# Layer 0 of a four-layer network: middle taps of ten images read from GpSimd-made copies moved by one element; two dummy products fewer after layer 1

## The chip, the core and the metric

The kernel runs on one core of a Trainium2 chip. The core has five engines that work side by side and wait for one another by semaphores: TensorE (PE in the profile, its weight loads PEld) multiplies matrices into PSUM, VectorE (DVE) and ScalarE (ACT) do elementwise work, GpSimd (POOL) does elementwise work in SBUF and issues DMAs, SyncE (SP) issues DMAs. The metric is the time of one execution on the device in microseconds (us); lower is better.

## The reference, cut to what matters

The input is 16 images of 256 channels, 28 x 28 pixels. Four layers follow one another. Layers 0 and 2 are of one kind: the sign of the input is convolved with the sign of the weights (3 x 3 taps, padding 1), and the result is normalized over all images.

```python
# layer 0
out = sign(x)                                   # the value of _binary_activation
y = conv3x3(out, sign(weights)) * mean(abs(weights))
yn = (y - mean(y)) * rsqrt(var(y) + EPS)        # over images and pixels
x = yn * gamma + beta + x
# layer 1: conv3x3 of sign(x), gates, conv1x1, residuals
# layer 2: x = prelu(bn(binconv2(sign(bn(prelu(binconv1(sign(bn(x)))))))) + x)
# layer 3: attention over the 784 pixels of each image, with a residual
```

The mean and the variance need every image, so a layer's normalization, and with it the next layer, can't start before the last image's convolution has ended.

## The kernel before

Each image lies in SBUF as 128 partitions x 2 channel groups x 784 pixels. sign_layer (L380) runs a signed convolution and is used three times: for layer 0 and for the two convolutions of layer 2. The two halves of the output channels are packed into one fp16 weight (a + 4095 b), so one pass of products yields both.

- sign_image (L424) has ScalarE write the signs of an image into fpads, a padded fp16 tile of 2 x 30 x 30 elements per partition, one of two such tiles in turn. Layer 0's sign0 (L520, instruction at L522) makes two instructions per image, one for each channel group, and then the next load of x is issued on SP.
- products (L390, matmuls at L400) runs over 6 chunks (2 channel groups x 3 rows of taps), the pieces of a block (two halves of 14 rows for a whole image) and the taps c = 0, 1, 2 of a row. The tap is where the read begins in a padded row: element c. So an image has 6 x 2 x 3 = 36 matmuls of 392 columns, and the read of the middle tap begins one 2-byte element into a row of 30.
- With the argument shifted, images from number direct on have the taps in another order: taps 0 and 2 of all chunks first, then the middle taps, which read the tile shifted at element 0. shifted is a copy of fpads moved on by one element, made by a DMA on SP in sign_image (L430). Layer 2 does this, with direct 4 in its first convolution and 2 in its second. Layer 0 gives no shifted tile, so all its taps read fpads.
- apart (L407) takes the packed result out of PSUM: ScalarE's L416 makes b, VectorE's L418 makes a. The result tile of layer 0 is n, 16-bit integers, two buffers in turn (room0). PSUM has three result buffers.
- post0 (L678) takes VectorE's statistics (L682) of the image before and stores n to DRAM (n0d) by a DMA on GpSimd (L684).
- steps are pieces of work that prepare the weights of the later layers. Two of them run beside each whole image, on ScalarE (L324, L343, L346, L588) and VectorE (L325, L577, L592 and the tensor operations recorded at L137).

The order of block j, written out by hand for PE, ScalarE, VectorE and SP, is: products of image j, sign_image of image j + 1, post of image j - 1, steps, apart of image j. GpSimd is not in that list; a planner orders its queue.

Layer 0's call is at L688. Its tiles come from the pool ph; the tag vs belongs to a tile of layer 1 (L717), which is first written after layer 0.

Between the layers PE runs keep_busy(n) (L498, matmuls at L502): n products of 512 columns on a tile of zeros that nobody reads. At the end of layer 1, after the last image's 1x1 convolution, the order is: ScalarE scales the convolution's result (L946), VectorE applies the prelu (L870), PE runs keep_busy(14) at L1175, then PE sums the gate's hidden layer (L709), ScalarE applies its bias (L893), PE makes the gate (L901), ScalarE the sigmoid (L902). VectorE makes layer 2's first variance from it (l_v), ScalarE its square root (L280), and with the result ScalarE writes the first signs of layer 2 (L1228).

Of the kernel before, what the change touches and what calls it, by code (L numbers as in the profile page):

```python
# [39 lines left out]
P = 128  # L40
B = 16
S = 28
# [7 lines left out]
PARTS = HALVES[:-1] + [(B - 1, r, HR // 2) for r in (HR, HR + HR // 2)]  # L50
# [36 lines left out]
def forward(ctx: ExitStack, tc: tile.TileContext, d: dict, out: bass.AP, careful: bool):  # L87
# [3 lines left out]
    nc = tc.nc  # L91
# [18 lines left out]
    SIGNS = FR if careful else F16  # L110

    def sign_pads(pool, tag):

        t = pool.tile([P, 2, 2, S + 2, S + 2], SIGNS, name="fpads", **({"tag": tag} if tag else {}))
        for i in (0, S + 1):
            for edge in (t[:, :, :, i:i + 1, :], t[:, :, :, :, i:i + 1]):
                nc.gpsimd.memset(edge.bitcast(F32) if careful else edge, 0.0)
        return t
# [14 lines left out]
    def vtile(name):  # L133
        return const.tile([P, 2], F32, name=name)

    def tt(o, a, b, op):
        V.tensor_tensor(o, a, b, op)  # L137
        return o
# [157 lines left out]
    def packed_weights(pool, **kw):  # L296
        return pool.tile([P, 6, 3, P], SIGNS, name="wpk", **kw)
# [66 lines left out]
    def whole_images(parts):  # L364

        return parts if careful else IMAGES + parts[2 * len(IMAGES):]

    def pieces(block):

        i, r0, rows = block  # L370
        return [(h, h * HR, HR) for h in range(2)] if rows == S else [(0, r0, rows)]

    def by_halves(ap, block):
        return halves(ap) if block[2] == S else ap

    def first_part(block):

        return 2 * block[0] + (block[1] >= HR) + (block[1] > HR)

    def sign_layer(pads, w, temp, room, sign, post, steps, moments, blocks, together=1, shifted=None, direct=2):  # L380

        pss = [None] * len(blocks)
        abs_ = [None] * len(blocks)

        groups = 2 if careful else 1
        size = 6 // groups

        def products(*js):  # L390
            for j in js:
                pss[j] = conv_ps()
            moved = shifted is not None and blocks[js[0]][0] >= direct
            for taps in ((0, 2), (1,)) if moved else ((0, 1, 2),):
                for n, (k, g) in enumerate(CHUNKS):
                    for j, (h, r0, rows) in ((j, p) for j in js for p in pieces(blocks[j])):
                        r = g + r0
                        for c in taps:
                            src, c0 = (shifted, 0) if moved and c == 1 else (pads, c)
                            T.matmul(  # L400
                                pss[j][:, n // size if careful else h, :rows * S].rearrange("p (a b) -> p a b", b=S),
                                lhsT=w[:, n, c, :], rhs=src[:, blocks[j][0] % 2, k, r:r + rows, c0:c0 + S],
                                start=(n % size == 0 and c == 0),
                                stop=(n % size == size - 1 and c == (1 if moved else 2)),
                            )

        def apart(j):  # L407
            for g in range(groups):
                n = blocks[j][2] * S
                t, ab = temp("t1")[:, :n] if careful else None, room(blocks[j], g)  # L410
                ps = pss[j][:, :, :HN] if blocks[j][2] == S else pss[j][:, g, :n]
                if careful:
                    A.activation(by_halves(t, blocks[j]), ps, AF.Identity, bias=rounding, scale=1.0 / PACK)
                    A.activation(ab[:, 1], t, AF.Identity, bias=unrounding)
                else:
                    A.activation(by_halves(ab[:, 1], blocks[j]), ps, AF.Copy, scale=1.0 / PACK)  # L416
                a, b = (by_halves(ab[:, mo], blocks[j]) for mo in range(2))
                V.scalar_tensor_tensor(a, b, -PACK, ps, ALU.mult, ALU.add)  # L418
                if g == 0:
                    abs_[j] = ab  # L420
                else:
                    tt(abs_[j], abs_[j], ab, ALU.add)

        def sign_image(i):  # L424

            for r0, r1 in ((0, HR + 1), (HR + 1, S)) if i == 0 else ((0, S),):
                load = sign(i, slice(r0, r1), lambda k: inner(pads[:, i % 2], k, r0, r1))
                if shifted is not None and i >= direct:
                    to, of = (t[:, i % 2].rearrange("p k a b -> p (k a b)") for t in (shifted, pads))
                    nc.sync.dma_start(out=to[:, 0:-1], in_=of[:, 1:])  # L430
                if load:
                    load()

        late = None
        gathered = False
        with tc.manual_schedule(engines={ET.PE, ET.Activation, ET.DVE, ET.SP}):
            sign_image(0)
            for j, block in enumerate(blocks):
                if j == 0:
                    products(*range(together))  # L440
                elif together <= j:
                    products(j)
                if block[1] == 0 and block[0] + 1 < B:
                    sign_image(block[0] + 1)
                after = post(blocks[j - 1], abs_[j - 1]) if j > 0 else ()
                if first_part(block) > EARLY and not gathered:
                    gathered = True
                    moments.gather()
                for p in range(len(pieces(block))):
                    if late:  # L450
                        late()
                    step = steps.pop(0) if first_part(block) + p >= 2 and steps else None
                    late = step() if step else None
                apart(j)
                for f in after:
                    f()
            post(blocks[-1], abs_[-1])
        assert not steps and not late

    def inner(pad, k, r0=0, r1=S):  # L460
        return pad[:, k, 1 + r0:1 + r1, 1:S + 1]
# [10 lines left out]
    def block_moments(name, blocks, summed=False):  # L472
        return Moments(name, EARLY, len(blocks) - EARLY, EARLY * HN, summed and not careful)

    sf0, sf1, sf2 = vtile("sf0"), vtile("sf1"), vtile("sf2")
    w0 = packed_weights(wpool, tag="wa")
# [13 lines left out]
    with tc.tile_pool(name="ps_conv", bufs=3, space=PSUM) as psc, \  # L490
            tc.tile_pool(name="ps_sm", bufs=2, space=PSUM) as pss:

        def conv_ps():
            return psc.tile([P, 2, 512], F32, tag="cv", name="cv")
# [3 lines left out]
        def keep_busy(n):  # L498

            ps = pss.tile([P, 512], F32, tag="sm", name="unused")  # L500
            for _ in range(n):
                tc.keep_in_program_order(T.matmul(ps, lhsT=idle[:, 0:P], rhs=idle, start=True, stop=True))  # L502

        with tc.tile_pool(name="ph1", bufs=1) as ph:

            fpads = sign_pads(ph, "vs") if careful else sign_pads(const, None)
            xs, ns = [None] * B, [None] * B

            def load_n(b):
# [16 lines left out]
            def temp(tag):  # L526
                return ph.tile([P, HN if careful else N], F32, tag=tag, name=tag, bufs=2)
# [24 lines left out]
            for step in signs:  # L552
                step.work()()

            pads = [
                const.tile([P, 2, S + 2, S + 2], BF16, tag=f"pad{i}", name=f"pad{i}") if careful
                else fpads[:, i].bitcast(BF16) for i in range(2)
            ]
# [62 lines left out]
            moved, b3c = vtile("moved"), vtile("b3c")  # L621
# [48 lines left out]
            steps = [constants]  # L670
# [14 lines left out]
                return ()  # L685

            mom = block_moments("l0", PARTS)
            sign_layer(fpads, w0, temp, room0, sign0, post0, steps, mom, whole_images(PARTS), together=2 if careful else 1)  # L688
            for b in range(2):
                xs[b] = None  # L690
                load_x(b)
# [25 lines left out]
            vs = ph.tile([P, 2, 4, 2, HR, S + 2], FR, tag="vs", name="vs")  # L717
# [231 lines left out]
            def unit_b(b, mo):  # L949
                prelu(us[b, mo], "f_alpha2", rf2, mo, sums_of(b + 2)[1][:, 1, mo:mo + 1])  # L950
# [163 lines left out]
            with tc.manual_schedule(engines={ET.PE, ET.DVE, ET.Activation, ET.SP}):  # L1114
# [57 lines left out]
                V.tensor_reduce(v1, sum_sq[:, :, 0:B - 1], AX.X, ALU.add)  # L1172
                unit_u(b, 1, last[:, 1, :])
                unit_b(b, 1)
                keep_busy(14)  # L1175
                for k in range(2):
                    squares(us[b, k], 0.0, sum_uu[:, k:k + 1], (B * N)**-0.5)
                h = hidden_b(B + 1, hidden_a(B + 1, px, TWO), TWO)
# [30 lines left out]
        with tc.tile_pool(name="ph2", bufs=1) as ph:  # L1209
            if careful:  # L1210
                w2b = packed_weights(ph, tag="wb")
            if careful:
                fpads = sign_pads(ph, "fpads")
# [88 lines left out]
            steps = []  # L1302
            if careful:
                steps = sign_weights(xpool, w2b, d["w2b"], ("x2", 3), tmp=ph)
# [5 lines left out]
                steps = [first_loads, None] + [t for s in load_ahead(steps, 2, now=False) for t in (None, None, s, None)]  # L1310
            shifted = None
            if not careful:
                shifted = ph.tile([P, 2, 2, S + 2, S + 2], SIGNS, name="shifted")
            mom = block_moments("l2b", PARTS, True)
            sign_layer(fpads, w2a, temp, room2, sign2a, post2(order, pv("a1"), mom, doubts[:, 2 * NB:3 * NB]), steps, mom, PARTS,
                       shifted=shifted, direct=4)
# [5 lines left out]
            mom = block_moments("l2c", PARTS, True)  # L1322
# [612 lines left out]
```

## Time and profile before

| what | value |
|---|---|
| median of 3 runs | 949.11 us (948.44 to 949.25) |
| the profiled execution | 949.33 us, span 947.5 us |
| granted clock of TensorE | 0.999 |
| layer 0's products on the chain | 15.71 to 107.71 us |
| layer 1 begins / ends on PE | 113.68 / about 457.9 us |
| layer 2's two convolutions | from 462.72 and 564.76 us |

The span runs from the first to the last instruction. Times in a timeline row are its start, counted from the span's start, and its length; in brackets stands how long the engine had been idle and what ended the wait. Rows of PE overlap, because matmuls are pipelined and their ends are modelled, so a matmul's pace is read from what waits for it, not from its own length.

### The profile page before, as it was taken

How to read it: one execution, taken by the hardware profiler on the slowest of the kernel's cores; microseconds unless marked ns; L12 is line 12 of the kernel's file. 1: busy time of each engine (PE TensorE's matmuls, PEld its weight loads, DVE VectorE, ACT ScalarE, POOL GpSimd, SP SyncE). 2: the span in 40 equal slices, each digit the busy share in tenths (PEclk: the TensorE clock that was granted, in tenths of full speed). 3: DMA queues.
4: the chain of work that ended last, by engine and by line, in shares of the span. 5: the costliest groups of instructions: out<-in, count | busy, mean ns of one | idle time of the engine just before them, and what ended most of it. 6: DMA issues, size and time to landing. Idle time of an engine off the chain costs nothing.

```text
span 947.5 us, 15043 instructions
## 1 busy us (share of the span) xinstructions
PE 930.7 (98%) x5636; PEld 583.2 (62%) x5636; DVE 757.1 (80%) x1446; ACT 675.1 (71%) x1179; POOL 139.0 (15%) x157
## 2 busy tenths in 40 slices
PE   7999999999999999999999999999999999999996
PEld 3555678788888878887555565556444444444442
DVE  3777798999998899987788878889656768687765
ACT  5665578888888888875777766775867666666652
POOL 2001100000000000000000000000334353534331
PEclk9999999999999999999999999999999999999999
DMA  9887434445533444421556211111132434434212
GB/s 346 287 303 264 168 121 138 165 181 198 198 139 139 148 156 164 160 86 50 223 209 214 113 40 59 79 78 59 35 68 70 112 92 94 112 78 126 69 68 106
DMA packets 39333, 130.70 MB, mean 138 GB/s; under 512 B 4866, under 2 KB 16324, under 8 KB 39252
## 3 DMA queue, kind: packets, MB, share of 16 engines
q1 hardware_dynamic: 33332, 98.31, 28.7%
q0 software_dynamic: 5632, 30.54, 11.7%
q8 instruction: 46, 0.75, 0.3%
q10 hardware_dynamic: 288, 0.80, 0.2%
q14 instruction: 35, 0.29, 0.1%
HBM read 72.67 MB, written 32.11 MB: 111 GB/s over the span
## 4 chain that ended last, share of the span: by engine, by line
PE 94%; DMA 1%; ACT 1%; DVE 1%; SPq 1%; issue 0%; DVEq 0%; ACTq 0%
PE cv L400 29%; PE cv L806 29%; PE sc L1498 8%; PE av L1519 8%; PE cv L933 5%; PE mi L1475 5%; PE sm L1561 2%; PE mi L1579 2%; PE unused L502 2%; PE sm L1519 1%; DMA xs<-in_x_dram 1%; PE gate L901 1%; PE hid L709 1%; DMA shifted<-fpads 1%; SPq L293 0%
## 5 line engine op out<-in xcount | busy, mean ns | idle before, releaser
L806 PE MATMUL cv<-vs,w 128*128 128x392 f32 (+1 forms) x1296 | 272.4, 352 | 0.3 <-DVE vs L137 0.3
L400 PE MATMUL cv<-fpads,wpk 128*128 128x392 f16 (+1 forms) x1458 | 247.8, 326 | 2.5 <-DVE wpk L325 1.2
L400 PEld LDWEIGHTS <-wpk 128*128 128x128 f16 x1782 | 171.5, 97 | 123.2 <-issue 3.1
L806 PEld LDWEIGHTS cv<-vs,w 128*128 128x128 f32 x768 | 143.2, 190 | 6.3
L1502 ACT ACTIVATE es<-sc 128x784 f32<-128x784 f32 x112 | 87.3, 822 | 41.4 <-PE sc L1498 41.4
L806 PEld LDWEIGHTS <-w 128*128 128x128 f16 x768 | 69.4, 99 | 51.9 <-issue 9.1
L1498 PE MATMUL sc<-q,keyswa 64*128 64x392 f32 x448 | 89.9, 513 | 0.9 <-ACT es L1502 0.9
L1519 PE MATMUL av<-es,v 128*64 128x392 f32 x448 | 80.7, 499 | 0.0
L1264 DVE SCALAR_TENSOR_TENSOR p<-ab,vec 128x392 f32<-128x392 int16 (+1 forms) x132 | 78.0, 605 | 0.0
L416 ACT ACTIVATE ab<-cv 128x392 int16<-128x392 f32 (+1 forms) x66 | 32.1, 486 | 56.3 <-PE cv L400 53.4
L1512 POOL TENSOR_TENSOR sum<-sum,es 128x784 f32<-128x784 f32 x32 | 67.2, 2099 | 3.1 <-ACT es L1502 0.6
L1498 PEld LDWEIGHTS sc<-q,keyswa 64*128 64x128 f32 x448 | 38.9, 186 | 44.0 <-issue 17.1
L400 PE MATMUL cv<-shifted,wpk 128*128 128x392 f16 (+1 forms) x324 | 60.6, 322 | 0.2 <-DMA shifted<-fpads 0.2
L806 PE MATMUL cv<-one_on,w 128*128 128x392 bf16 x240 | 59.4, 329 | 0.0
L961 POOL DMA_DIRECT2D x2d<-x x16 | 8.6, 536 | 345.3 <-DVE x L955 285.0
L1486 DVE COPY keyswa<-mi 64x392 f32<-64x392 f32 x31 | 16.3, 564 | 53.1 <-ACT q L1482 53.1
L1519 PEld LDWEIGHTS av<-es,v 128*64 128x64 f32 x448 | 29.4, 136 | 47.4 <-issue 47.0
L418 DVE SCALAR_TENSOR_TENSOR ab<-ab,cv 128x392 int16<-128x392 int16 (+1 forms) x66 | 36.0, 546 | 27.7 <-ACT ab L416 27.3
L788 ACT CAST vs<-vs 128x840 fp32r<-128x840 bf16 x63 | 54.1, 882 | 2.5 <-DVE vs L137 2.5
L933 PE MATMUL cv<-z,fw 128*128 128x392 f32 x256 | 48.9, 342 | 0.1
L933 PEld LDWEIGHTS cv<-z,fw 128*128 128x128 f32 x256 | 46.1, 188 | 0.9 <-ACT z L925 0.9
L1475 PE MATMUL mi<-p,wqk 128*128 128x392 f32 x124 | 45.1, 506 | 0.1
(323 smaller groups left out, 1531.2 us busy)
## 6 DMA issues: line engine op xcount, KB each, us to landing
xs<-in_x_dram SPq DMA_DIRECT2D x30, 784.0 KB, 5.1
one_on<-vs SPq DMA_DIRECT2D x60, 209.8 KB, 2.8
x2d<-x POOLq DMA_DIRECT2D x16, 784.0 KB, 3.6
out_dram<-p SPq DMA_DIRECT2D x15, 784.0 KB, 3.4
shifted<-fpads SPq DMA_DIRECT2D x26, 449.8 KB, 2.8
p<-x2d POOLq DMA_DIRECT2D x14, 784.0 KB, 6.7
p<-x2d SPq DMA_DIRECT2D x13, 784.0 KB, 5.7
n0d<-n POOLq DMA_DIRECT2D x16, 392.0 KB, 4.8
```

Source lines behind the costliest of these rows:

```text
L400: T.matmul(pss[j][:, n // size if careful else h, :rows * S].rearrange("p (a b) -> p a b", b=S), lhsT=w[:, n, c, :], rhs=src[:, blocks[j][ ...
L416: A.activation(by_halves(ab[:, 1], blocks[j]), ps, AF.Copy, scale=1.0 / PACK)
L418: V.scalar_tensor_tensor(a, b, -PACK, ps, ALU.mult, ALU.add)
L788: copy(v, w)
L806: T.matmul(ps.rearrange("p (a b) -> p a b", b=S), lhsT=w[:, k, c, u, mo * P:(mo + 1) * P], rhs=one_on[:, u, k, :, 0:S] if moved and c == 1 ...
L933: T.matmul(ps[:, h, :HN], lhsT=w[:, k, mo * P:(mo + 1) * P], rhs=z2[b][:, k, h * HN:(h + 1) * HN], start=(k + i == 0), stop=(k + i == 2),)
L1264: V.scalar_tensor_tensor(p, y, alpha[:, mo:mo + 1], y, ALU.mult, ALU.max, accum_out=mom.sums_at(at, mo)[0] if mom.by_sums(at, mo) else None,)
L1475: T.matmul(ps[:, h, :HN], lhsT=wqk[:, k, :], rhs=x[b][:, k, h * HN:(h + 1) * HN], start=(k == 0), stop=(k == 1))
L1498: T.matmul(ps[:, h, :HN], lhsT=chunk[rows], rhs=qs[b][rows], start=True, stop=True)
L1502: A.activation(e, ps[:, :, :HN], AF.Exp, scale=0.125)
L1512: (V if late else nc.gpsimd).tensor_tensor(sums[b, late], sums[b, late], e, ALU.add)
L1519: T.matmul(ps[64 * h:64 * h + 64, :HN], lhsT=w, rhs=e[:, h, :], start=start, stop=stop)
```

## The change

sign_layer gets two arguments: until, which ends the run of images with moved copies, and copy, the operation that makes the copy. Layer 0 gets a tile moved0 for two images (in the buffer of tag vs), direct stays 2, until is 12, and copy is GpSimd's tensor_copy. So for images 2 to 11 GpSimd copies 1799 fp16 elements per partition from fpads to moved0, moved on by one, after ScalarE's signs of that image, and the image's matmuls run with taps 0 and 2 first and the middle taps last, from moved0. Images 0, 1 and 12 to 15 stay as they were. Layer 2 keeps its DMAs. The keep_busy(14) at L1175 becomes keep_busy(12).

```diff
-    def sign_layer(pads, w, temp, room, sign, post, steps, moments, blocks, together=1, shifted=None, direct=2):
+    def sign_layer(pads, w, temp, room, sign, post, steps, moments, blocks, together=1, shifted=None, direct=2, until=B, copy=nc.sync.dma_start):
...
-            moved = shifted is not None and blocks[js[0]][0] >= direct
+            moved = shifted is not None and direct <= blocks[js[0]][0] < until
...
-                if shifted is not None and i >= direct:
+                if shifted is not None and direct <= i < until:
                     to, of = (t[:, i % 2].rearrange("p k a b -> p (k a b)") for t in (shifted, pads))
-                    nc.sync.dma_start(out=to[:, 0:-1], in_=of[:, 1:])
+                    copy(out=to[:, 0:-1], in_=of[:, 1:])
...
             fpads = sign_pads(ph, "vs") if careful else sign_pads(const, None)
+            moved0 = None if careful else ph.tile([P, 2, 2, S + 2, S + 2], SIGNS, tag="vs", name="moved0")
...
-            sign_layer(fpads, w0, temp, room0, sign0, post0, steps, mom, whole_images(PARTS), together=2 if careful else 1)
+            sign_layer(fpads, w0, temp, room0, sign0, post0, steps, mom, whole_images(PARTS), together=2 if careful else 1,
+                       shifted=moved0, until=12, copy=nc.gpsimd.tensor_copy)
...
-                keep_busy(14)
+                keep_busy(12)
```

The other path of the kernel (careful), which runs only if the fast path's own watch says so, has no moved copies.

## The prediction

> **What bounds the kernel now.** I read the page first (busy times, chain that ended last), then the chain in order of time, then three stretches of the timeline: ScalarE in layer 0, ScalarE in layer 2, and all engines between layers 1 and 2. Last I read GpSimd's groups.
>
> ```profile
> PE 930.7 (98%) x5636; PEld 583.2 (62%) x5636; DVE 757.1 (80%) x1446; ACT 675.1 (71%) x1179; POOL 139.0 (15%) x157
> PE 94%; DMA 1%; ACT 1%; DVE 1%; SPq 1%; issue 0%; DVEq 0%; ACTq 0%
> 15.71 92.00 PE cv L400 x558
> ```
>
> TensorE is the chain. Layer 0's convolution (L400) lies on it without a break for 92 us, so whatever shortens those matmuls shortens the kernel, as long as nothing else becomes late.
>
> The pace per image is read from ScalarE's first reading of each result (L416), where its idle time is ended by PE. Layer 0, images 7 to 10:
>
> ```profile
> 58.74 0.82 ACT L416 ACTIVATE n<-cv 128x784 int16<-128x784 f32 x1 [1.21 <-PE cv L400]
> 59.47 1.60 ACT L522 ACTIVATE fpads<-xs 128x784 f16<-128x784 f32 x2
> 64.86 0.82 ACT L416 ACTIVATE n<-cv 128x784 int16<-128x784 f32 x1 [3.80 <-PE cv L400]
> ...
> 70.98 0.82 ACT L416 ACTIVATE n<-cv 128x784 int16<-128x784 f32 x1 [0.79 <-PE cv L400]
> ...
> 77.11 0.82 ACT L416 ACTIVATE n<-cv 128x784 int16<-128x784 f32 x1 [3.08 <-PE cv L400]
> ```
>
> An image takes 6.12 us (64.86 to 70.98, 70.98 to 77.11). Layer 2's second convolution has the same shapes, its middle taps read from a moved copy:
>
> ```profile
> 583.07 0.50 ACT L416 ACTIVATE ab<-cv 128x392 int16<-128x392 f32 x1 [1.38 <-PE cv L400]
> ...
> 589.04 0.50 ACT L416 ACTIVATE ab<-cv 128x392 int16<-128x392 f32 x1 [1.38 <-PE cv L400]
> ...
> 595.01 0.50 ACT L416 ACTIVATE ab<-cv 128x392 int16<-128x392 f32 x1 [1.38 <-PE cv L400]
> ```
>
> There an image (two halves) takes 5.97 us. In layer 2's first convolution the halves before image 4 take 3.05 to 3.06 us and those after it 2.99: the step falls at the image where the copies begin.
>
> For the dummy products, the end of layer 1:
>
> ```profile
> 454.75 3.20 PE L502 MATMUL unused<-idle 128*128 128x512 bf16 x14
> 457.88 0.39 PE L709 MATMUL hid<-g,se 128*64 128x1 f32 x4
> 458.31 0.25 ACT L893 ACTIVATE hidden<-hid,seb 32x1 f32<-32x1 f32 x1 [0.29 <-PE hid L709]
> 459.45 1.28 ACT L1188 ACT_TABLE_LOAD   x1
> 459.46 0.16 DVE L137 TENSOR_TENSOR dqg<-gates,s_bn 128x2 f32<-128x2 f32 x1
> 460.50 0.16 DVE L137 TENSOR_TENSOR l_v<-l_v,l_w 128x2 f32<-128x2 f32 x1
> 460.85 0.19 ACT L280 ACTIVATE l2a_t<-l_v 128x2 f32<-128x2 f32 x1
> ```
>
> **What the Trainium skill says.** "TensorE: Matmul & The Clock Gate", section "Wait — 56ns, not 53.3ns?": a warm matmul of N columns takes N / 2.4 GHz plus about 2.5 ns. For 392 columns that is 165.8 ns; layer 2's moved image is 5970 / 36 = 165.8 ns, so the trace agrees, and a moved image has nothing left to gain. Layer 0's is 6122 / 36 = 170.1 ns. The page gives no reason for this; the trace's step at image 4 puts it on the middle tap, which starts one 2-byte element in. "SBUF — State Buffer", section "Who interferes with whom": a VectorE instruction with two SBUF inputs, or in a two-port mode, excludes a GpSimd instruction that reads SBUF, and whichever starts first keeps the ports for its whole length. GpSimd does almost nothing in layer 0 before, so no row here shows it. "GPSIMD Engine Reference", section "3.1 Elementwise — side-by-side cycle accounting", prices a tight one-input loop at 1.8 cycles of 1.2 GHz per element; this is used below.
>
> **Part 1, the middle taps.** An image has 36 matmuls (6 chunks, 3 taps, 2 halves) before and after. In the 10 images 2 to 11, twelve each change their source and come last in the image. Saving per image: 6.122 - 5.970 = 0.152 us. Ten images: 1.52 us, all on the chain. Bounds: 170.1 to 165.8 is the whole distance to the skill's rate, so 1.55 at most with rounding; if the last-digit differences between layers count (6.11 in layer 2 unmoved), 1.4.
>
> **Part 1, the copies.** Ten GpSimd copies of 128 x 1799 fp16 are added, one per image. No such copy is in the trace. From below, GpSimd's memsets of 128x896 and 128x448 take 0.856 and 0.467 us, 0.87 ns per element: 1799 x 0.87 + 0.08 = 1.64 us. The skill's 1.8 cycles give 2.7 us (estimate). From above, GpSimd's two-input sum over 784 elements takes 2.099 us, 2.68 ns per element: 4.8 us. I take 2.5 us. A copy can't gain anything by itself, so nothing lies below 1.64.
>
> When is it needed? The ScalarE signs for image 9 end at 61.07 (59.47 + 1.60), while image 8 runs from about 58.7. At the new pace image 9's middle taps begin at 58.7 + 5.97 + 2/3 x 5.97 = 68.65: 7.6 us for the copy. The tightest case is image 6: ScalarE waited for a weight transfer until 40.31, so its signs end at 44.42, and image 6 would start at about 45.9 (46.5 less four images' gain); middle taps at 49.9, 5.5 us for the copy. So 1.64, 2.7 and 4.8 us are all hidden. If that cover were gone, each microsecond beyond it would be PE idle.
>
> Behind the copy on GpSimd stands the store of the image before last (n0d, 0.54 us to issue, 4.7 us median to landing). It now issues at 60.87 just before the copy could start; behind it, it issues at about 61.07 + 2.5 = 63.6 and lands at 68.3. Its buffer is next written by ScalarE's L416 of image 9, at about 70.8 at the new pace relative to the same signs. 2.5 us remain; the longest landing of 7.9 us would hold ScalarE for 0.7 us, whose next signs have more than 3 us to spare.
>
> VectorE shares ports: per image some 1.6 us of its work has two SBUF inputs or a two-port form (L137, L325, L577, L592) and may wait for one copy. VectorE is busy 72% between 46 and 82 us (26 of 36 us), and a result buffer of TensorE comes free two images before it is needed. I cost this at nothing. SP's queue loses and gains nothing: the copies don't go through it, and the loads behind each sign keep their place. The copy's tile uses layer 1's vs buffer, first written after 113 us, long after image 11.
>
> **What shifts with it.** Before image 13's L416 (95.47) ScalarE waits 3.80 us for PE, so the tail of layer 0 and the norm after it follow PE. They move 1.52 us earlier together, with the loads of n for layer 1.
>
> **Part 2, two dummies.** They free 2 x 0.216 = 0.43 us of PE (14 in 3.0 us). hid waits on the dummies only: its input was ready at 457.42 (DVE, 457.26 + 0.16), it started at 457.88. With 12 it starts near 457.5. ScalarE's square holds L893 until 458.02, so L893 gains 0.29 at most. VectorE gains nothing: its long product keeps it until 459.46, when dqg starts anyway, and l_v is there at 460.66 as before. The table load starts 0.29 earlier, but L280 then waits for l_v: about 460.69 instead of 460.85. Gain 0.16 us; bounds 0 and 0.43. What is late next is VectorE's l_v.
>
> **Sum.** 1.52 + 0.16 = 1.68 us. The profiled execution took 949.33 us (span 947.5, 1.8 around it), so 947.65 for it; the median of the runs, 0.22 lower, gives 949.11 - 1.68 = **947.43 us**, 0.18% faster.
>
> A measurement of this kernel can tell about 0.2% (1.9 us) from no change, so the forecast sits just on the near side of that line, at 947.21.
>
> **The rivals.**
> - A2, the dummies give all of their 0.43: 1.52 + 0.43 = 1.95, 947.15. For it: hid and its followers do wait for them. Against: VectorE's unbroken product.
> - B, the port lock takes the place of the odd tap: VectorE's L137 and L577 wait for copies, ScalarE's L588 for them, and signs come late where they have little room (image 6 has 1.5 us to its start). Two such places at 0.5 us each: 948.4. Against: the weight steps are spread out and most signs end over 3 us early.
> - C, the odd start is not what costs in layer 0: the second image of layer 2's second convolution also has a 2.99 us half (571.05 to 574.04) unmoved. With half the gain: 0.76 + 0.16, 948.2. Against: the clean step at image 4.
> - D, slower: GpSimd becomes the bound. Its period is copy + 0.54 us for the store; beyond 5.97 us per image, from a copy of 5.43 us (3.0 ns per element) on, it paces TensorE. At 6.0 us: 0.57 x 9 = 5.1 us, less the 1.6 us of head start left at the first image, is 3.5 us of PE idle: 949.11 - 1.68 + 3.5 = 950.9; at 7 us (1.57 x 9 - 0.6) it is about 961. For it: fp16 on GpSimd is in no row, and locks with VectorE add to each copy. Against: even the two-input rate gives 4.8.
> - E, fewer dummies let TensorE's clock drop before layer 2: one stretch of 3.4 us at half rate (the skill's window, "The HAM clock gate (the "warmup" mystery)" on the TensorE page, an estimate) costs 1.7 us and gives 949.1. Against: idle gaps there stay under 0.5 us.
>
> **How the numbers follow.** A, the sum as it stands, 0.64; A2 0.12; B 0.06; C 0.06; D 0.09; E 0.03. A's own range is 946.9 to 947.9 (first term 1.4 to 1.55, second 0 to 0.3, medians to 0.3); some 45% of it lies beyond 947.21. Faster: 0.29 + 0.11 = 0.40. Slower: D and part of E and of what I didn't see, 0.12. Within 0.2%: 0.48. The range runs from 946.8 to 948.6 and leaves out D, E and the edges, under 2 in 10.
>
> **What would show it.** Right: L416 at 5.97 us spacing for images 2 to 11 and 6.12 after; L400 from shifted copies with no idle ended by POOL; copies of 1.6 to 2.7 us; signs of layer 1 (112.26) 1.5 us earlier; hid right after g, L280 right after l_v. Wrong: PE idle ended by the copy (D), signs late behind L588 (B), 6.05 us spacing without idle (C), a granted clock under 1 at layer 2's start (E).

## The result, and the profile after

| | before | changed |
|---|---|---|
| median of 22 runs each | 948.89 us (948.44 to 950.08) | 947.49 us (947.02 to 948.83) |
| the profiled execution | 949.33 us, span 947.5 | 947.43 us, span 945.6 |
| layer 0's products on the chain | 92.00 us | 90.63 us |
| the first dummy product to L280 | 6.10 us | 5.95 us |

The ratio is 0.9985, with a 95% interval of 0.9979 to 0.9990. The change takes away 1.40 us, which is inside the 0.2% that a measurement of this kernel can tell from no change, though its interval leaves out 1. In the code after, layer 0's lines stand one further down (L522 is L523, L418 is unmoved), and those after layer 0's call two further (L1228 is L1230).

First the chain of the changed kernel in order of time: start, length, engine, tile and line.

```profile
15.85 90.63 PE cv L400 x558
...
106.51 0.34 ACT n L416
...
111.03 0.96 ACT fpads L764
```

Layer 0 is still an unbroken run of matmuls. It has the same 558 pieces as before and is 1.37 us shorter. Layer 1's first signs (L764) begin at 111.03 instead of 112.26, although the run of products began 0.14 us later than before: the tail of the layer moved with it.

The pace, from ScalarE's timeline of the changed kernel, for four of the ten images:

```profile
58.07 0.82 ACT L416 ACTIVATE n<-cv 128x784 int16<-128x784 f32 x1 [0.26 <-PE cv L400]
64.05 0.82 ACT L416 ACTIVATE n<-cv 128x784 int16<-128x784 f32 x1 [3.66 <-PE cv L400]
70.04 0.82 ACT L416 ACTIVATE n<-cv 128x784 int16<-128x784 f32 x1 [0.65 <-PE cv L400]
76.02 0.82 ACT L416 ACTIVATE n<-cv 128x784 int16<-128x784 f32 x1 [2.94 <-PE cv L400]
```

Each idle stretch is ended by PE, so the starts tell PE's pace: three images in 17.95 us, 5.984 us each, where it was 6.122. Images 12 and 13 are at 6.12 again. So 0.138 us per image, not 0.152. The matmuls' own starts in the traces show where it comes from: before, the matmul after a middle tap begins 176 to 178 ns after it, all others 165 to 170 ns after theirs; in the changed kernel 165 to 170 ns is all there is (read between 46 and 76 us before, 58 and 81 us after).

The copies, from the view of the tile moved (duration minimum, median and maximum in ns; first and last start in us):

```profile
L400 PE MATMUL cv<-moved,wpk x120: 327/328/332, 26.0 to 81.6; 128*128 128x392 f16 x120
L430 POOL COPY moved<-fpads x10: 1697/1697/1847, 19.1 to 72.7; 128x1799 f16<-128x1799 f16 x10
```

A copy takes 1.70 us, 0.94 ns per element. No matmul is listed as waiting for one. Where it stands in GpSimd's queue, from GpSimd's timeline:

```profile
60.20 0.54 POOL L685 DMA_DIRECT2D n0d<-n  x1 [2.87 <-DVE n L418]
60.73 1.70 POOL L430 COPY moved<-fpads 128x1799 f16<-128x1799 f16 x1
```

The planner put the store of n ahead of the copy, not behind it. So the copy waits for the store, and the store for VectorE's L418. Nine of the ten copies begin where a store ends; the one at 24.55 waits for its signs alone.

The port lock is in the trace. First two lines of the kernel before, then the timeline of the changed kernel around image 1:

```profile
24.20 0.43 DVE L137 TENSOR_TENSOR asm<-st 128x256 f32<-128x256 f32 x1
...
25.12 0.75 ACT L588 ACTIVATE w<-asm 128x256 f16<-128x256 f32 x2 [0.48 <-DVE asm L137]
```

```profile
24.55 1.85 POOL L430 COPY moved<-fpads 128x1799 f16<-128x1799 f16 x1 [3.72 <-ACT fpads L523]
24.88 1.78 DVE L137 TENSOR_TENSOR asm<-st 128x256 f32<-128x256 f32 x1
...
27.16 0.75 ACT L589 ACTIVATE w<-asm 128x256 f16<-128x256 f32 x2 [1.86 <-DVE asm L137]
...
29.92 0.80 ACT L416 ACTIVATE n<-cv 128x784 int16<-128x784 f32 x1
```

VectorE's operation on asm (two inputs in SBUF) took 0.43 us before; here it begins after the copy (24.55), ends at 26.66, just after the copy's end at 26.40, and takes 1.78. ScalarE then waits 1.86 us for it, where it had waited 0.48, and reads image 2's result at 29.92, not 28.15. This is the Trainium skill's "SBUF — State Buffer", section "Who interferes with whom": whichever instruction starts first keeps the shared ports for its whole length. The trace agrees (1.78 us against 0.43). How much of it there is, from the busy times by stretch (before, then after; the columns are the stretch, its length, and busy time of PE, PEld, DVE, ACT and POOL, then clock, DMA share and GB/s):

```profile
46.00:86.00 40.00, 40.00 (x237) 22.93 (x236) 28.38 (x56) 25.54 (x44) 4.07 (x8) 1.00 0.79 285
```

```profile
46.00:86.00 40.00, 40.00 (x242) 23.25 (x241) 32.67 (x60) 26.59 (x46) 14.24 (x17) 1.00 0.83 290
```

VectorE is 4.3 us busier here, in part because more of its work falls into the stretch (60 instructions instead of 56), while PE stays at 40.00 of 40: none of the held time reaches TensorE here. Over the whole execution VectorE is busy for 762.9 us, in the kernel before for 757.1.

Between layers 1 and 2, the timeline of the changed kernel:

```profile
456.42 0.36 PE L711 MATMUL hid<-g,se 128*64 128x1 f32 x4
456.89 0.25 ACT L895 ACTIVATE hidden<-hid,seb 32x1 f32<-32x1 f32 x1
...
457.35 1.03 DVE L969 SCALAR_TENSOR_TENSOR product<-x,shift,last 128x784 f32<-128x784 f32 x1
...
458.03 1.28 ACT L1190 ACT_TABLE_LOAD   x1
...
459.35 0.16 DVE L137 TENSOR_TENSOR l_v<-l_v,l_w 128x2 f32<-128x2 f32 x1
...
459.55 0.20 ACT L280 ACTIVATE l2a_t<-l_v 128x2 f32<-128x2 f32 x1
```

The table load is over at 459.31 and L280 starts at 459.55, as soon as VectorE's l_v is there. Before, the load ended at 460.73, after l_v, and L280 followed the load. The chain now runs through VectorE's two products (L969), which the dummies used to hide.

### The profile page after: what moved, and what is told of

It reads as the page before. It is cut to its first block, busy times and chain, and to the rows that moved or that the text cites. A ratio compares the mean times of both kernels' runs of the same rounds, so it can differ in the third digit from the quotient of the medians.

```text
span 945.6 us, 15054 instructions
## 1 busy us (share of the span) xinstructions
PE 928.5 (98%) x5628; PEld 583.0 (62%) x5634; DVE 762.9 (81%) x1446; ACT 675.5 (71%) x1179; POOL 156.0 (16%) x167
## 4 chain that ended last, share of the span: by engine, by line
PE 95%; DVE 1%; ACT 1%; DMA 1%; SPq 1%; issue 0%; DVEq 0%; ACTq 0%
PE cv L400 30%; PE cv L808 29%; PE sc L1500 9%; PE av L1521 8%; PE cv L935 5%; PE mi L1477 5%; PE sm L1563 2%; PE mi L1581 2%; PE unused L502 2%; PE sm L1521 1%; DMA xs<-in_x_dram 1%; PE gate L903 1%; PE hid L711 1%; ACT es L1504 0%; SPq L293 0%
## 5 line engine op out<-in xcount | busy, mean ns | idle before, releaser
L400 PE MATMUL cv<-fpads,wpk 128*128 128x392 f16 (+1 forms) x1338 | 228.1, 324 | 2.6 <-DVE wpk L325 1.2
L416 ACT ACTIVATE ab<-cv 128x392 int16<-128x392 f32 (+1 forms) x66 | 32.1, 486 | 56.0 <-PE cv L400 53.1
L418 DVE SCALAR_TENSOR_TENSOR ab<-ab,cv 128x392 int16<-128x392 int16 (+1 forms) x66 | 36.1, 547 | 27.4 <-ACT ab L416 26.2
```

The lines of the kernel that those rows point to most:

```text
L400: T.matmul(pss[j][:, n // size if careful else h, :rows * S].rearrange("p (a b) -> p a b", b=S), lhsT=w[:, n, c, :], rhs=src[:, blocks[j][ ...
```

## The experiments

All times are medians, each against the kernel before in the same session. Chain and pace are those of one profiled execution.

### The two parts apart

**Copies only.** The changed kernel with the dummies back.

```diff
-                keep_busy(12)
+                keep_busy(14)
```

> The changed kernel with 14 dummy products again: the copies alone. Layer 0's products on the chain should take 90.6 us as in the changed kernel (92.0 before), and the stretch from the dummies (PE) to layer 2's first product 7.9 to 8.0 us as before. My sum of two parts: 1.4 us below before. If the whole gain came from the dummies and the rest were noise: equal to before.

Measured: 947.57 us against 949.00, ratio 0.9983 (0.9977 to 0.9990). Products on the chain 90.63 us; first dummy to L280 6.10 us, as in the kernel before.

**Dummies only.** The kernel before with two dummies fewer.

```diff
-                keep_busy(14)
+                keep_busy(12)
```

> The kernel before with 12 dummy products: 0.15 us below before, read in the trace as L280 starting 5.95 us after the first dummy and not 6.10; the chain there then runs through VectorE's products. If all of their 0.43 us counted (rival A2): 5.67 us and 0.43 below before. If the clock dropped (rival E): a granted clock under 1 after 462 us and up to 1.7 us above before.

Measured: 948.78 us against 949.00, ratio 0.9998 (0.9989 to 1.0006). Products 92.00 us; first dummy to L280 5.95 us, and the granted clock 0.998. The trace separates the parts cleanly: 1.37 us from the first, 0.15 from the second. By its time alone the second can't be told from nothing.

### Is it the odd start, and do the copies cost anything?

**Aligned, no copy.** The middle taps of images 2 to 11 read fpads at element 2, in the changed kernel's order, and nothing is copied. This computes the middle taps with the pixel to the right.

```diff
-                            src, c0 = (shifted, 0) if moved and c == 1 else (pads, c)
+                            src, c0 = (shifted, 0) if moved and c == 1 and until == B else (pads, 2 if moved and c == 1 else c)
...
-                       shifted=moved0, until=12, copy=nc.gpsimd.tensor_copy)
+                       shifted=moved0, until=12, copy=lambda out, in_: None)
```

> No copies; the middle taps of images 2 to 11 come last and read fpads at element 2 instead of 1 (so they use the pixel beside the right one; the output differs). It shows an even start without anything that a copy costs. If the odd start is the cost and the copies are free: 5.98 us per image as in the changed kernel, and the same time as it. If GpSimd's reads take a little from TensorE: 5.97 us per image, 0.14 us less than the changed kernel. If the copies' holds on VectorE cost something later: more than 0.2 us less.

**Order only.** The same, but the middle taps stay at element 1 of fpads. Only the order of the taps is new.

```diff
-                            src, c0 = (shifted, 0) if moved and c == 1 else (pads, c)
+                            src, c0 = (shifted, 0) if moved and c == 1 and until == B else (pads, c)
```

> No copies; the taps in the new order (0 and 2 first, then the middle ones), the middle taps still read fpads at element 1. If the odd start is the cost: 6.12 us per image and 0.15 us (the dummies alone) below before. If the new order makes the gain (rival C's family): 5.98 us per image and 1.4 us below before.

Measured: aligned 947.38 us (ratio 0.9982, 0.9975 to 0.9989), order only 948.86 us (0.9998, 0.9990 to 1.0006). The chain of the aligned kernel:

```profile
15.66 90.63 PE cv L400 x558
```

ScalarE's timeline of the kernel with the order alone:

```profile
60.07 0.82 ACT L416 ACTIVATE n<-cv 128x784 int16<-128x784 f32 x1 [1.22 <-PE cv L400]
66.20 0.82 ACT L416 ACTIVATE n<-cv 128x784 int16<-128x784 f32 x1 [3.81 <-PE cv L400]
72.33 0.82 ACT L416 ACTIVATE n<-cv 128x784 int16<-128x784 f32 x1 [0.79 <-PE cv L400]
```

At an even start the products take 90.63 us with the copies or without them, so one copy per image costs nothing on the path. VectorE is busy for 757.2 us without them, so the ten copies hold it for 5.7 us. At the odd start an image takes 6.13 us in the new order too. The two kernels differ in the start alone (element 2 or 1), so the start is the cause: 0.138 us over 12 middle-tap matmuls, 11.5 ns each.

### How much copying is hidden?

**Each copy three and four times.** GpSimd's copying is tripled and quadrupled (the second has range(4)), where rival D had put the limit at 5.43 us for the copies of an image.

```diff
-                       shifted=moved0, until=12, copy=nc.gpsimd.tensor_copy)
+                       shifted=moved0, until=12, copy=lambda out, in_: [nc.gpsimd.tensor_copy(out=out, in_=in_) for _ in range(3)])
```

> Each copy made three times over (3 x 1.70 = 5.1 us, with the store's 0.54 a GpSimd period of 5.64 us per image, under TensorE's 5.98). If only GpSimd's own pace can hurt (rival D): no PE idle ended by POOL, and the changed kernel's time within 0.2 us. If the port lock is what bites (rival B): VectorE's two-input instructions grow to 1 to 5 us, ScalarE's signs come late, and PE waits for them: more than 0.5 us above the changed kernel.

> Each copy made four times over (6.8 us, period 7.34 us, over 5.98). By rival D's reckoning PE loses 7.34 - 5.98 = 1.36 us per image for 9 images, 12.2 us, less a head start of 0.5 to 2 us at the first: PE idle of 10 to 12 us ended by POOL, 957 to 959 us. If GpSimd had slack that I don't see, or TensorE could run on with its three result buffers: under 952 us.

Measured: 966.21 us with three (ratio 1.0182, 1.0168 to 1.0196) and 983.78 us with four (1.0366, 1.0352 to 1.0380). Rival B's sign came, longer two-input operations on VectorE and a loss of more than 0.5 us, but no sum here had foreseen its size, and TensorE waits for the copies themselves. (Of the second, 3.9 us come after its last piece of work, as in the next experiment.) Waits of layer 0 with three copies (engine and line, who ended the wait, total us, times, longest):

```profile
PE cv L400 <- POOL moved L690: 13.2, 7, 3.2
ACT w L589 <- DVE st L578: 12.7, 5, 4.3
ACT w L589 <- DVE asm L137: 9.6, 6, 3.5
```

The timeline of that kernel shows one turn of the loop:

```profile
58.78 0.59 POOL L685 DMA_DIRECT2D n0d<-n  x1
...
59.36 5.35 POOL L690 COPY moved<-fpads 128x1799 f16<-128x1799 f16 x3
...
61.38 3.61 DVE L137 TENSOR_TENSOR asm<-asm,st 128x256 f32<-128x256 f32 x2
...
65.02 0.42 ACT L589 ACTIVATE w<-asm 128x256 f16<-128x256 f32 x1 [1.40 <-DVE asm L137]
...
65.65 0.80 ACT L416 ACTIVATE n<-cv 128x784 int16<-128x784 f32 x1
...
66.48 0.97 DVE L418 SCALAR_TENSOR_TENSOR n<-n,cv 128x784 int16<-128x784 int16 x1 [1.50 <-ACT n L416]
...
67.75 0.54 POOL L685 DMA_DIRECT2D n0d<-n  x1 [3.04 <-DVE n L418]
...
73.69 2.16 PE L400 MATMUL cv<-moved,wpk 128*128 128x392 f16 x12 [2.21 <-POOL moved L690]
```

The three copies leave the ports only in short gaps, so VectorE's two operations on asm take 3.61 us instead of 0.76. ScalarE waits for them at L589 and reads the image's result late (L416); L418 is late; the store waits for L418, and the next copies stand behind the store. GpSimd then idles for 3.04 us, though its own work (5.35 + 0.54) would fit into 5.98 us. The next three copies end at 73.64, and TensorE has waited 2.21 us for them: a loop over four engines, not GpSimd's pace.

These waits are not the whole loss. From its first L416 to its last, layer 0 takes 108.2 us in this trace and 90.1 in the changed kernel. Of the 18.1 us between them, 13.2 are TensorE's waits for copies (the first line of the table), and some 3.4 are matmuls that ran slowly after two of these waits. One of the two:

```profile
51.15 3.36 PE L400 MATMUL cv<-moved,wpk 128*128 128x392 f16 x12 [1.99 <-POOL moved L690]
```

Twelve such matmuls take 2.16 us elsewhere. In both places the trace has some eleven matmuls in a row that begin 326 or 327 ns apart instead of 165 to 170, and the granted clock is 0.91 from 26 to 66 us. So TensorE ran at half its pace there, as rival E feared for another place. After the five other waits it did not, and what decides this isn't shown.

**Two memsets ahead of one copy.** As long on GpSimd, but only the copy reads SBUF.

```diff
-                       shifted=moved0, until=12, copy=nc.gpsimd.tensor_copy)
+                       shifted=moved0, until=12, copy=lambda out, in_: (nc.gpsimd.memset(out, 0.0), nc.gpsimd.memset(out, 0.0), nc.gpsimd.tensor_copy(out=out, in_=in_)))
```

> Two memsets of the copy's size ahead of each single copy, in place of two further copies: GpSimd is held for about 5.0 us per image as with three copies, but reads SBUF for 1.7 us only. If the port lock made the loss with three copies: VectorE's two-input instructions have their lengths of the changed kernel, and the time is within 1 us of it (947 to 948.5). If GpSimd's own pace and its queue behind the store made it: PE idle ended by POOL as there, about 966 us.

Measured: 951.08 us, ratio 1.0021 (1.0012 to 1.0029). Layer 0 is not what got longer. From its chain, the products and the last piece of work:

```profile
15.74 90.63 PE cv L400 x558
...
939.14 0.07 DVE p L1592
```

The products are as in the changed kernel, and so is the end: there too the last piece is at 939.14. But the span is 949.4 us instead of 945.6. The extra 3.8 us come after all work, while the program leaves. The page's row of one queue of instruction fetches shows one packet more (changed kernel, then this one):

```profile
q14 instruction: 35, 0.29, 0.1%
```

```profile
q14 instruction: 36, 0.29, 0.1%
```

Of the 14 kernels, two have 36 packets there, this one and the one with four copies, and in these two the span ends 10.2 and 10.3 us after the last piece of work on the chain; in the others it is 6.4 to 7.0. Both added instructions to GpSimd's program (20 and 30). That the further fetch is the cause is read from this agreement, not tested; the kernel with three copies also has 20 more and doesn't show it. Taken off (an estimate), 951.08 becomes 947.3, the changed kernel's time.

So 5.0 us of GpSimd work per image and the store of 0.54 do fit, as D's count had it, if they are not three copies in a row. What makes the difference isn't fully told apart. The memsets need no signs, and the planner let them run ahead of the store, so only one copy stands behind it; and they hold VectorE far less. Its busy time over the whole execution is 757.2 us without copies, 762.9 with one per image, 767.2 with two memsets and one, and 786.0 with three copies. Beside memsets the operations with two inputs keep their length, but L578 does not, twice:

```profile
34.91 3.57 POOL L690 MEMSET moved<- 128x1799 f16 x2
35.33 1.61 DVE L578 TENSOR_SCALAR st<-st 128x768 f32<-128x768 f32 x1
```

It takes 0.55 us alone. A kernel that tells the two differences apart, the place in the queue and the held ports, was not run.

### Other ways and places for the copies

**By DMA on SP,** as layer 2 does it.

```diff
-                       shifted=moved0, until=12, copy=nc.gpsimd.tensor_copy)
+                       shifted=moved0, until=12)
```

> The copies of images 2 to 11 by DMA from SP, as layer 2 makes them, GpSimd left out. If only the even start matters and the copy is in time: 90.6 us of products and the changed kernel's time. VectorE's holds go (24.0 and 28.4 us busy in 16 to 46 and 46 to 86 us as before). If the transfers, on engines already 80 to 90% busy there, come late or delay the loads of x: PE idle ended by DMA, up to 1 us above.

Measured: 949.49 us, ratio 0.9999 (0.9991 to 1.0007). Busy times by stretch of this kernel, columns as above, and its waits:

```profile
46.00:86.00 40.00, 38.25 (x229) 22.01 (x228) 28.62 (x58) 24.56 (x43) 4.05 (x8) 1.00 0.99 364
```

```profile
ACT sg L324 <- DMA st<-in_w2a_dram: 4.2, 1, 4.2
DVE st L578 <- DMA st<-in_w_dram: 3.8, 1, 3.8
...
PE cv L400 <- DMA moved<-fpads: 1.7, 2, 1.1
```

VectorE has no holds (28.62 us busy, as before), but the DMA engines are at 0.99 of their time instead of 0.79 before. Weight transfers land late, ScalarE waits for them, signs and copies follow, and PE idles for 1.75 us of the 40. At the median the whole gain is lost. But the thirteen executions run from 947.60 to 951.80 us, and the profiled one is the slowest: the trace shows how time is lost in a bad execution, and the best is as fast as the changed kernel.

**More images.** Copies for images 2 to 15, 1 to 15 and 1 to 13.

```diff
-                       shifted=moved0, until=12, copy=nc.gpsimd.tensor_copy)
+                       shifted=moved0, until=B, copy=nc.gpsimd.tensor_copy)
...
+                       shifted=moved0, direct=1, until=B, copy=nc.gpsimd.tensor_copy)
...
+                       shifted=moved0, direct=1, until=14, copy=nc.gpsimd.tensor_copy)
```

> Copies for images 2 to 15. Four images more at 0.138 us: 0.55 us below the changed kernel (90.1 us of layer 0's products on the chain), if VectorE keeps up at the tail. If the copies' holds on VectorE delay the last images' statistics: the products shrink to 90.1 us all the same, but the stretch from the last product to layer 1's first signs grows from 4.5 us by the holds, up to 1.7 us, and the time is equal to the changed kernel or above it.

> Copies for images 1 to 15. One image more than in the last run: 0.14 us below it if the copy of image 1 (its signs are made beside image 0, which ends near 16.2 us) is there before image 1's middle taps near 20 us; if it isn't, PE idle ended by POOL near 20 us.

> GpSimd copies for images 1 to 13, none in the last two. Two terms: three images more than the changed kernel at 0.138 us, and a tail from the last product to layer 1's first signs as long as there (4.55 us) because VectorE is free of holds by then: 0.41 us below it, about 947.1, near the run for images 1 to 15 or below. If the tail is longer all the same: equal to the changed kernel.

| images with copies | median us | ratio (95%) | products, us | last L416 to layer 1's signs, us |
|---|---|---|---|---|
| 2 to 11 (the change) | 947.49 | 0.9985 (0.9979 to 0.9990) | 90.63 | 4.52 |
| 2 to 15 | 947.37 | 0.9988 (0.9979 to 0.9996) | 90.16 | 4.89 |
| 1 to 15 | 946.96 | 0.9982 (0.9975 to 0.9988) | see below | 4.62 |
| 1 to 13 | 947.40 | 0.9984 (0.9978 to 0.9991) | 90.31 | 4.53 |

With images 12 to 15 the products end another 0.47 us sooner, and 0.37 of it is given back. The chain of the kernel with images 2 to 15:

```profile
15.71 90.16 PE cv L400 x558
...
105.93 3.54 DMA n<-n0d
```

Here the end of the layer waits for an image of n read back from DRAM, which in the changed kernel lay off the chain. With images 1 to 15 the chain passes through VectorE near the end, so its products can't be read in one piece; from the first L416 (16.09) to layer 1's signs (110.18) it takes 94.09 us against 94.58 in the changed kernel. That is the lowest median, 0.53 us under the change, but the intervals overlap, and no more is claimed for it. With images 1 to 13 the products shrink by 0.32 us, not by the 0.41 expected, with a tail as long as in the change, and the median can't be told from the change's.

### Why 0.138 and not 0.152

**By halves.** The changed kernel with layer 0's images worked in two halves, as layer 2 does.

```diff
-            sign_layer(fpads, w0, temp, room0, sign0, post0, steps, mom, whole_images(PARTS), together=2 if careful else 1,
+            sign_layer(fpads, w0, temp, room0, sign0, post0, steps, mom, PARTS, together=2 if careful else 1,
```

> The changed kernel with layer 0's images in halves, as layer 2 runs them, instead of whole. My sum took layer 2's 5.970 us per image, the changed kernel shows 5.984. If working on two PSUM banks in turn costs the 0.014: 2.985 us per half. If it is layer 0 itself (its DMA traffic): 2.992 per half. The time may be up to 1 us above the changed kernel, for ScalarE and VectorE have more instructions.

Measured: 950.08 us, ratio 1.0010 (1.0003 to 1.0016). ScalarE's timeline of this kernel, every fourth half:

```profile
49.21 0.50 ACT L416 ACTIVATE n<-cv 128x392 int16<-128x392 f32 x1 [0.97 <-PE cv L400]
...
61.15 0.50 ACT L416 ACTIVATE n<-cv 128x392 int16<-128x392 f32 x1 [0.56 <-PE cv L400]
...
73.10 0.50 ACT L416 ACTIVATE n<-cv 128x392 int16<-128x392 f32 x1 [0.58 <-PE cv L400]
```

Two moved images take 11.94 us, 5.97 each, the pace of layer 2. An unmoved half takes 3.05 to 3.06 us here, 6.11 per image, not 6.12. So whole images run about 0.014 us slower than two halves in the moved order, and about 0.01 in the old one. In a whole image the two halves' products alternate within each chunk and write two parts of PSUM in turn; that is the difference in form, but which feature of it costs was not tried. The higher time comes from the beginning: the first image ends 2.6 us later (19.04 instead of 16.45), since each half needs all six chunks of the weights, which arrive during that image.

## Why the prediction was right, point by point

**Part 1, the middle taps.** The mechanism holds, and C falls: with aligned starts and no copies the whole gain is there, with the odd start none of it. The 2.99 us half that spoke for C is a matter of when ScalarE read it: the next half's first matmul begins 3.055 us after that half's own (570.786 to 573.841 in the trace before), as with the unmoved half ahead of it. The term was mis-sized: "6.122 - 5.970 = 0.152" set a whole image against two halves. Like for like it is 0.138, so 1.38 for ten images against 1.37 on the chain. The clue had been on the table: the lower bound of 1.4 took layer 2's unmoved 6.11. "A moved image has nothing left to gain" fails by the same 0.014. The Trainium skill's "TensorE: Matmul & The Clock Gate", section "Wait — 56ns, not 53.3ns?", gives 165.8 ns for 392 columns; 5984 / 36 is 166.2 ns, slightly above it.

**Part 1, the copies.** 2.5 us was taken, 1.70 measured, close to the low bound of 1.64 from the memset rows. The 1.8 cycles per element of the Trainium skill's "GPSIMD Engine Reference", section "3.1 Elementwise — side-by-side cycle accounting", gave 2.7. The same section has 1.03 cycles for the shortest loop bodies, which would give 1.54 us (an estimate); this copy takes 1.13 cycles of 1.2 GHz. It was hidden, as said.

**GpSimd's order.** Wrong. The text had the store behind the copy; the planner put it ahead. With one copy this costs nothing. With three it is part of the loop described above.

**VectorE's ports, costed at nothing, and B.** Right for the time, since with and without copies the products take 90.63 us. But the holds were no small thing: 5.7 us of VectorE's time, and a ScalarE 1.8 us late at image 2. B's mechanism is real and its price here nil. In one point the prediction read its source too narrowly. The Trainium skill's "SBUF — State Buffer", section "Who interferes with whom", limits the lock to GpSimd instructions that read SBUF only where VectorE has two inputs; VectorE in a two-port mode contends with GpSimd as such. The memsets agree: beside them L578, which the prediction counted with the two-port forms, took 1.61 us instead of 0.55.

**Part 2.** 0.16 predicted, 0.15 measured, alone and together with part 1. l_v is what is late next, as said. A2 falls, since L280 gained only what VectorE left. E falls too: from the start of layer 2's first convolution to that of its second it is 102.05 us (461.43 to 563.48), and it was 102.04 before, so no stretch ran at half rate.

**D.** It did not happen, since the copy takes 1.70 us. But its threshold, "from a copy of 5.43 us on", was wrong in kind: 5.35 us of copies already cost 18.7 us against the changed kernel, through held VectorE, ScalarE, L418 and the store, and through a slower TensorE after the waits.

**The sum.** 1.68 predicted; 1.52 in the two places of the trace, 1.40 in the medians. That 947.43 came within 0.06 us of the measured 947.49 is in part luck: the gain was put 0.28 us too high, and it was taken from a median of three runs that lay 0.22 us above that of 22, so two errors nearly cancel. The spans differ by 1.9 us, more than the two parts explain; the rest lies in single waits of one execution, such as 0.20 us of PE idle in layer 2 for a late copy in the profile before, and isn't put down to the change.

## What to carry to other kernels

- A 392-column matmul whose fp16 rows begin at an odd element ran 11.5 ns longer here; a copy moved by one element removes that if the copy has somewhere to hide. When such a gain is estimated from another layer, compare blocks of the same shape.
- Copying on GpSimd beside a busy VectorE has a limit in the shared ports and in what stands ahead of it in the queue, well before GpSimd itself is full. Ask who waits for VectorE's held operations, and whether that chain leads back to the next copy.
- A gain on the main chain isn't a gain at the stage's end: the tail waits for other engines and transfers, and the last images bring least.

## What the runs showed of the hardware that wasn't expected

- Copies in a row on GpSimd starve VectorE out of proportion: one copy per image held it for 5.7 us in all, three for 28.8, and two operations on asm went from 0.76 to 3.61 us in the turn shown.
- A memset on GpSimd, which reads nothing, can hold a VectorE operation too: L578 (one input) took 1.61 us beside it instead of 0.55, in two places of one trace.
- After waits of 3.18 and 1.99 us, some eleven matmuls in a row began 327 ns apart instead of about 166, in the kernel with three copies; after five other waits, of 0.46 to 2.21 us, they did not.
- The time from the last piece of work to the end of the span was 6.4 to 7.0 us in twelve kernels and 10.2 to 10.3 us in two, with one instruction packet more in those two. A difference of 0.4% between two kernels can lie wholly behind their last piece of work.
